# A four-layer graph network: where layer 2's load buffers lie, and what its first two chunks begin with

## The chip, the cores and the metric

The kernel runs on one core of one Trainium2 chip. The metric is the device time of the whole program in microseconds (us), as a median over runs. The kernel before has a median of 1073.51 us over 3 runs (1072.81 to 1073.6).

The engines are named as in the profile: PE (TensorE), DVE (VectorE), ACT (ScalarE), POOL (GpSimd) and SP (SyncE, which here issues most DMAs). Each engine works through its own instructions in order; semaphores tie the engines together.

## The reference

`x` is 2708 x 128 and `adj` is 2708 x 2708, both float32; about 0.6% of `adj` is not zero. Each of the four layers normalises the rows of `x`, applies a ReLU to give `h`, and adds a graph layer to `x`. Layers 0 and 1 are a mean over neighbours and a message network with GELU for each edge. The layers that the change touches are 2 and 3:

```python
# layer 2
agg = adj @ states                       # states is h
msg = relu(agg @ W_msg.T + b_msg)
x = x + gru_cell(msg, states)            # gates r, z and candidate n
# layer 3, for each of two heads
mask = (adj > 0) | eye(n)
h = x_norm @ ff0_w[i].T
e = where(mask, leaky_relu(s_src[:, None] + s_dst[None, :]), NEG)
att = softmax(e, axis=1) @ h + x
```

## The kernel before, in words

The 2708 rows are held as 22 row tiles of 128 rows (`NT = 22`; the last has 20). Columns are taken in chunks of four tiles, 512 columns (`GROUPS`: five of these and one of 148 columns).

**Layer 0** reads `adj` once, lists the non-zero values of each row (`val`, `col`) and writes the transposed matrix to `adjT` in DRAM. **Layer 1** works from the lists: `period(t)` handles row tile t, with gathers by matmul, a GELU, and sums; `updates` (line 697) does the steps that end a group of four tiles, up to `hs`, the normalised rows that layer 2 multiplies. Its memory is held by pools that are open until `lists.close()`: `val`, `col`, `later`, `xb` and others in `keep`, scratch in `fix`, `once` and more. The order of instructions in layer 1 and in layer 2 is that of the code (`manual_schedule`). After layer 1's last update, DVE works out from the lists whether any row had more entries than the lists hold (`lost1`, `over1`, `many`), and puts that into `flag`.

**Layer 2** is `aggregate` and `finish_chunk`. For each chunk of columns, `aggregate` is called for pieces of five row tiles (`PIECE = 5`: four pieces of 1.28 MB, and a last one of the remaining two tiles, 256 KB and 40 KB). It loads the piece from `adjT` on SP's queue (L1082, L1084) into one of three buffers `a2` of pool `l2a`; lets DVE make the mask (`a > 0`, kept for layer 3) of the first four row tiles (L1086) and POOL that of the fifth (L1089); and gives PE one matmul for each row tile into the PSUM sum `p_agg` (L1094). A fourth load can be issued only when both masks and the matmuls of the first piece have been done.

`finish_chunk` is a generator. It copies the sum (`aggc`, L1105), turns `h` (`p_h2`, `hc`), puts the diagonal into the mask (L1112, four DVE operations), and does the GRU: p_m and `msg` (L1115, L1117), p_hn and `half_n` (L1121, L1123), the gates (L1125 to L1130), p_in (L1131), `nn` on DVE and ACT (L1134 to L1138), `y2` on DVE (L1142 to L1144), p_y back to rows (L1150) and into `xs` (L1156), two layer norms (`n3`, whose `h` rows ACT scales at L137, and `n3z`, `z`), p_z (L155, L1171) and p_hv, `hv` (L1179, L1185). Its pool `l2g` has one buffer for each tag, and `aggc` shares tag `t2` with `nn`, `half_n` shares `t1` with `y2`. The sums lie in PSUM tags acc0 and acc1 in turn, the gates in acc2 to acc5.

When a chunk's sum is done, `follow(finish_chunk(...))` hands the generator to a small planner. Each matmul of `aggregate` spends `n / CH` units of a clock (1 for 512 columns); `advance()` lets each generator run on when the units that it yielded have passed. So the finishing of one chunk is laid, at build time, between the matmuls of the next. `late_weights` (L379 to L388, among it p_w on PE and `w_x` on DVE) runs after the first chunk's sum.

**Layer 3** takes `row`, `hv`, `lift` and the mask, weighs on DVE (L923) and multiplies on PE (L955). Its tiles (pool `l3`) are allocated right after `lists.close()`; a first instruction on POOL is the memset of `score` (L887).

Of the kernel before, what the change touches and what calls it, by code (L numbers as in the profile page):

```python
# [20 lines left out]
F32 = mybir.dt.float32  # L21
BF16 = mybir.dt.bfloat16
AF = mybir.ActivationFunctionType
ALU = mybir.AluOpType
AX = mybir.AxisListType
U16 = mybir.dt.uint16
I32 = mybir.dt.int32
U8 = mybir.dt.uint8
PSUM = bass.MemoryType.PSUM

P = 128
N = 2708
D = 128
NT = (N + P - 1) // P
FULL = N // P
TAIL = N - FULL * P
CH = 512
# [7 lines left out]
NB = (N + JB - 1) // JB  # L45
S = 8
E = P
GROUPS = [(t, min(4, NT - t)) for t in range(0, NT, 4)]
# [3 lines left out]
def size(t):  # L52
    return min(P, N - t * P)
# [7 lines left out]
def listed_layers(ctx: ExitStack, tc: tile.TileContext, x, adj, w, out, flag):  # L61
    nc = tc.nc
# [100 lines left out]
    keep = lists.enter_context(tc.tile_pool(name="keep", bufs=1))  # L163
    val = keep.tile([P, NT, NB, S], F32, name="val")
    col = keep.tile([P, NT, NB, S], U16, name="col")
    own = keep.tile([P, NT], F32, name="own")
    total = keep.tile([P, NT], F32, name="total")
    inv = keep.tile([P, NT], F32, name="inv_deg")

    HB = NB // 2  # L170
    HP = 8
    R = 4
    C = 4 * S + R + 1

    count = keep.tile([P, P], F32, name="count")
    nc.gpsimd.iota(count, [[1, P]], base=0, channel_multiplier=0, allow_small_or_imprecise_dtypes=True)
# [9 lines left out]
    rows_n = keep.tile([P, NT, NB], BF16, name="rows_n")  # L186
    ends = keep.tile([P, NT, NB], BF16, name="ends")
    some4 = keep.tile([P, 4, NB, S], BF16, name="some4")
    later = keep.tile([P, NB, E], BF16, name="later")
    nc.gpsimd.memset(later, 0.0)  # L190
    xb = [keep.tile([P, NB, C], BF16, name=f"xb{q}") for q in range(2)]
    for q in range(2):
        nc.gpsimd.tensor_copy(xb[q][:, :, 4 * S : 4 * S + R], part.unsqueeze(1).to_broadcast([P, NB, R]))

# [184 lines left out]
    def late_weights():  # L379
        nc.vector.tensor_tensor(gate_b, b_ih[:, 0:2], b_hh[:, 0:2], ALU.add)  # L380
        nc.vector.tensor_scalar(gate_b, gate_b, 0.5, None, ALU.mult)
        nc.vector.tensor_scalar(half_b, b_hh[:, 2:3], 0.5, None, ALU.mult)
        nc.vector.tensor_copy(w_x[:, 0 : 2 * D], ff0T)
        for k in range(2):
            p = bank("p_w")[:, 0:2]
            nc.tensor.matmul(p, ff0[:, k, :], attn[:, 2 * k : 2 * k + 2], start=True, stop=True)
            nc.vector.tensor_copy(w_x[:, 2 * D + k : 2 * D + k + 1], p[:, 1:2])
            nc.vector.tensor_copy(w_x[:, 2 * D + 2 + k : 2 * D + 3 + k], p[:, 0:1])  # L388
# [6 lines left out]
    with (  # L395
# [56 lines left out]
        def list_late(t):  # L452
            units = state.pop(("late", t), [])
            for n, b, a in units:
                nc.vector.max(val[0 : size(n), n, b, :], a)
            for n, b, a in units:
                nc.vector.max_index(col[0 : size(n), n, b, :], val[0 : size(n), n, b, :], a)
# [251 lines left out]
        def period(t, between=()):  # L709

            now, c, b, a = (0 <= t + q < NT for q in range(4))
            last = 0 <= t - 1 < NT
            if c and not between:
                put_values(t + 1)
            for k in range(GB):
                for step in between[k : k + 1]:
                    step()
                if now:
                    combine(t, k)
                    activate(t, k)  # L720
                if k < 2:
                    if last:
                        gather(t - 1, GB - 2 + k)
                    if k == 0 and c:
                        pass_on(t + 1)
                    if k == 1 and a:
                        rank(t + 3)
                    if k == 1 and last:
                        close_tile(t - 1)
                elif now:  # L730
                    gather(t, k - 2)
                if k in (1, 2) and b:
                    fetch(t + 2, k - 1)
                if k == 1 and a:
                    describe(t + 3)
                if k == 2:
                    if now and t % 2 == 0 and t + 2 < NT:
                        sources(t // 2 + 1)
                    if a:
                        select_rows(t + 3)  # L740
                    if now and t + 4 < NT:
                        count_rows(t + 4)
                    updates(t)
                if k > 0 and c:
                    put_more(t + 1, k)
                if k == 3 and c:
                    columns(t + 1)
                if k == 3 and b:
                    place(t + 2)
                if k == 4 and a:  # L750
                    finish_rows(t + 3)
                if k == 4:
                    load_late(t + 1)
                if k == GB - 1:
                    list_late(t)


        def spread_sums(g):
# [63 lines left out]
        def put_rest(t):  # L822
            for k in range(1, GB):
                put_more(t, k)

        with tc.manual_schedule():
            for step, n in (
                (spread_sums, 0), (spread_sums, 1), (rank, 0), (enter, 0),
                (select_rows, 0), (describe, 0), (enter, 1), (spread_sums, 2), (rows, 0), (turn_rows, 0),
                (rows, 1), (destinations, 0), (turn_rows, 1),  # L830
                (finish_rows, 0), (fetch_both, 0), (rank, 1), (enter, 2), (spread_sums, 3), (select_rows, 1),
                (split_destinations, 0), (destinations, 1), (describe, 1), (rows, 2), (turn_rows, 2),
                (place, 0), (pass_on, 0), (sources, 0), (enter, 3), (spread_sums, 4), (split_destinations, 1),
                (destinations, 2), (rows, 3), (turn_rows, 3), (finish_rows, 1), (fetch_both, 1), (enter, 4),
                (spread_sums, 5), (columns, 0), (place, 1), (split_destinations, 2), (destinations, 3), (rows, 4),
                (turn_rows, 4), (enter, 5), (rank, 2), (select_rows, 2), (rows, 5), (turn_rows, 5), (describe, 2),
                (split_destinations, 3), (put_values, 0), (destinations, 4), (put_rest, 0), (finish_rows, 2),
            ):
                step(n)

            def fourth():
                split_destinations(4)
                destinations(5)

            def fifth():
                split_destinations(5)
                put_values(1)

            period(0, (fourth, fifth))
            for t in range(1, NT + 1):  # L850
                period(t)
            for t in range(NT + 1, NT + 1 + STEPS):
                updates(t)


        lost = fix.tile([P, 3, NT], F32, name="lost1")
        nc.vector.reduce_sum(lost[:, 0, :], rows_n, AX.X)
        nc.vector.tensor_scalar(lost[:, 1, :], own, 0.0, None, ALU.is_gt)
        nc.vector.tensor_scalar(lost[:, 2, :], own, 0.0, None, ALU.is_lt)
        nc.vector.tensor_tensor(lost[:, 0, :], lost[:, 0, :], lost[:, 1, :], ALU.add)  # L860
        nc.vector.tensor_tensor(lost[:, 0, :], lost[:, 0, :], lost[:, 2, :], ALU.subtract)
        nc.vector.tensor_tensor(lost[:, 0, :], lost[:, 0, :], total, ALU.not_equal)
        nc.vector.reduce_sum(flag, lost[:, 0, :], AX.X)
        over = fix.tile([P, 2], F32, name="over1")
        many = once.tile([P, NT, NB], BF16, tag="picked", name="many")
        nc.vector.tensor_tensor(many, ends, rows_n, ALU.add)
        nc.vector.tensor_scalar(many, many, float(E), None, ALU.is_gt)
        nc.vector.reduce_sum(over[:, 0:1], many, AX.XY)
        nc.vector.tensor_scalar(many, val[:, :, :, S - 1], 0.0, None, ALU.is_gt)
        nc.vector.reduce_sum(over[:, 1:2], many, AX.XY)  # L870
        for q in range(2):
            nc.vector.tensor_tensor(flag, flag, over[:, q : q + 1], ALU.add)
    lists.close()


# [1 line left out]

    l3 = ctx.enter_context(tc.tile_pool(name="l3", bufs=1))  # L880
    h3 = l3.tile([P, NT, D], F32, name="h3")
    mask = l3.tile([P, NT, N], U8, name="mask")
    hv = l3.tile([P, NT, 2, D + 1], F32, name="hv")
    lift = l3.tile([P, NT, 2], F32, name="lift")
    row = l3.tile([P, 2, N], F32, name="row")
    score = l3.tile([P, NT, 4], F32, name="score")
    nc.gpsimd.memset(score[:, NT - 1, :], 0.0)  # L887
    ident_8 = l3.tile([P, P], U8, name="ident_8")
    nc.vector.tensor_copy(ident_8, ident)
    PIECE = 5  # L890
    RUNS = ((0, 3), (3, 8), (11, 8), (19, 3))
# [175 lines left out]
            yield apart  # L1067

    with (
        tc.tile_pool(name="l2a", bufs=3) as apool,  # L1070
        tc.tile_pool(name="l2g", bufs=1) as pool,
        tc.tile_pool(name="l2z", bufs=2) as zpool,
        tc.tile_pool(name="l3v", bufs=4) as vpool,
# [26 lines left out]
        def finish_chunk(t0, k0, pa):  # L1100
# [103 lines left out]
            for k in range(2):  # L1204
# [2 lines left out]
                    passed[k * k0 : (k + 1) * k0, :].rearrange("t i -> (t i)")[0:n].partition_broadcast(P),  # L1207
                )

        for g, (t0, k0) in enumerate(GROUPS):  # L1210
            pa = accs.tile([P, CH], F32, tag=f"acc{g % 2}", name="p_agg")
            for j0 in range(0, NT, PIECE):
                aggregate(t0, k0, pa, j0)
            if t0 == 0:
                late_weights()
            follow(finish_chunk(t0, k0, pa))
            advance()
        last = RUNS[0]
# [486 lines left out]
```

## Time and profile before

| | |
|---|---|
| median of 3 runs | 1073.51 us (1072.81 to 1073.6) |
| span of the profiled execution | 1069.6 us |
| median less that span | 3.9 us |
| PE busy in the span | 950.0 us (89%) |
| DVE, ACT, POOL busy | 824.4, 515.4, 398.7 us |
| layer 1's last update matmul (p_u) ends | 614.87 us |
| layer 2's matmuls (p_agg) | 620.98 to 774.0 us |
| mean granted clock of PE | 0.943 |

The profile gives no time of the profiled execution other than its span, from the first to the last instruction; the 3.9 us is the part of the median that lies outside of it, if that execution took as long as the median.

How to read what follows: a line of the waits names the engine and line that waited, what it waited for, the total, how often, and the longest. A line of the timeline begins with start and duration, and ends with the idle time before it and its releaser. A line of the stretches gives length, busy time of PE, PE's weight loads, DVE, ACT and POOL with the number of records, then the granted clock of PE, the share of the DMA engines, and GB/s. A float32 matmul of 512 columns appears as two records.

### The profile page before, as it was taken

Reading aid. Unit: us, or ns where it says so; the run is one execution under the profiler, and the core shown is the slowest. Engines: PE = TensorE matmul, PEld = TensorE weight load, DVE = VectorE, ACT = ScalarE, POOL = GpSimd, SP = SyncE. Lnnn points to the kernel's source line nnn. Section 1 sums busy time; section 2 is a strip of 40 time slices with the busy share of each in tenths; the row PEclk is TensorE's granted clock in tenths of the full one; section 3 lists DMA queues with packets and bytes.
Section 4 is the critical chain, followed back from the end, with each engine's and each line's share of the span. In section 5 each row is a group of like instructions: output and inputs, shape, how many; then the busy total and the mean of one; then the engine's idle time right before and its main releaser. Section 6 shows DMA issues by size and latency. Waiting matters only on the chain. (4 is left out here: it accounts for less than half of the span.)

```text
span 1069.6 us, 21992 instructions
## 1 busy us (share of the span) xinstructions
PE 950.0 (89%) x7950; PEld 754.1 (71%) x7950; DVE 824.4 (77%) x2853; ACT 515.4 (48%) x1428; POOL 398.7 (37%) x476
## 2 busy tenths in 40 slices
PE   5798889934799999999999979999978999999993
PEld 2454445433799999899899934444578999999772
DVE  7999999768577798787878265666578977997673
ACT  7777777634766666666666522433321200320142
POOL 3311112022776656666766163343410300430132
PEclk9999999766799999999999979999989999999996
DMA  9888996221233433322221075566300000000000
GB/s 365 315 303 316 316 342 243 78 65 46 88 109 106 124 95 106 106 91 83 97 96 57 28 256 186 185 225 216 91 22 26 9 1 1 6 15 1 2 15 14
DMA packets 60625, 129.67 MB, mean 121 GB/s; under 512 B 11160, under 2 KB 23828, under 8 KB 57798
## 3 DMA queue, kind: packets, MB, share of 16 engines
q1 hardware_dynamic: 58690, 125.38, 34.2%
q10 hardware_dynamic: 1816, 2.80, 0.8%
q8 instruction: 64, 1.05, 0.4%
q14 instruction: 55, 0.45, 0.1%
HBM read 81.55 MB, written 30.87 MB: 105 GB/s over the span
## 5 line engine op out<-in xcount | busy, mean ns | idle before, releaser
L955 PE MATMUL att<-hv,wt 128*128 128x129 f32 (+2 forms) x1936 | 243.8, 283 | 8.7 <-DVE wt L923 8.7
L955 PEld LDWEIGHTS att<-hv,wt 128*128 128x128 f32 (+2 forms) x1936 | 224.7, 192 | 25.8 <-DVE wt L923 10.1
L923 DVE SCALAR_TENSOR_TENSOR wt<-row,lift,mask 128x1024 f32<-128x1024 f32 (+5 forms) x176 | 160.3, 939 | 34.9 <-PE att L955 34.8
L536 POOL TENSOR_SCALAR put<-mine,value 128x128 f32<-128x128 bf16 x176 | 149.8, 867 | 70.3 <-DVE mine L433 67.9
L612 PE MATMUL p_m<-s,sel 128*128 128x128 bf16 x1452 | 161.6, 220 | 5.4 <-ACT g L624 5.4
L616 PE MATMUL p_m<-d,cols 124*128 124x128 bf16 (+1 forms) x1452 | 161.7, 220 | 1.4 <-DVE cols L566 1.3
L121 POOL TENSOR_TENSOR n_r<-n_r,minus_half 128x4 f32<-128x4 f32 (+1 forms) x31 | 46.1, 1486 | 286.5 <-DVE n_r L120 280.9
L637 PE MATMUL agg<-put,g 128*128 128x128 f32 (+1 forms) x968 | 135.9, 281 | 0.0
L297 PE MATMUL acc<-a,hs 128*128 128x512 f32 (+2 forms) x264 | 124.4, 574 | 10.8 <-ACT hs L137 10.8
L309 PEld LDWEIGHTS p_T<-ident,a 128*128 128x128 f32 x484 | 60.1, 144 | 88.3 <-issue 40.3
L637 PEld LDWEIGHTS agg<-put,g 128*128 128x128 f32 x968 | 118.2, 192 | 0.0
L1094 PE MATMUL p_agg<-a,hs 128*128 128x512 f32 (+2 forms) x264 | 109.3, 556 | 7.3 <-DMA a<-adjT 7.2
L612 PEld LDWEIGHTS <-sel 128*128 128x128 bf16 x1452 | 104.3, 98 | 10.8 <-issue 7.0
L285 DVE FIND_INDEX8 col<-val,a 128x8 uint16<-128x124 f32 (+1 forms) x400 | 108.1, 285 | 0.0
L309 PE MATMUL p_T<-ident,a 128*128 128x128 f32 x484 | 82.3, 289 | 26.2 <-ACT aT L313 19.4
L624 ACT ACTIVATE g<-p_m 128x512 f32<-128x512 f32 x132 | 73.1, 554 | 63.8 <-PE p_m L616 63.8
L616 PEld LDWEIGHTS <-cols 124*128 124x128 bf16 (+1 forms) x1452 | 102.5, 98 | 1.9 <-DVE cols L566 1.9
L544 ACT ACTIVATE put<-mine,value 128x128 f32<-128x128 bf16 x308 | 100.5, 391 | 0.0
L283 DVE MAX8 val<-a 128x8 f32<-128x124 f32 (+1 forms) x400 | 92.8, 276 | 2.5 <-DMA a<-in_adj 2.5
L313 ACT ACTIVATE aT<-p_T 128x512 f32<-128x512 f32 (+2 forms) x132 | 71.1, 541 | 47.9 <-ACT aT L313 32.7
L1094 PEld LDWEIGHTS p_agg<-a,hs 128*128 128x128 f32 (+1 forms) x264 | 47.5, 194 | 55.8 <-issue 54.2
L297 PEld LDWEIGHTS acc<-a,hs 128*128 128x128 f32 (+1 forms) x264 | 44.7, 202 | 25.9 <-issue 14.8
(252 smaller groups left out, 1418.7 us busy)
## 6 DMA issues: line engine op xcount, KB each, us to landing
a<-in_adj SPq DMA_DIRECT2D x21, 1354.0 KB
adjT<-aT SPq DMA_DIRECT2D x105, 256.0 KB
a<-adjT SPq DMA_DIRECT2D x20, 1280.0 KB
spread<-passed SPq DMA_DIRECT2D x22, 704.0 KB
later<-sel SPq DMA_DIRECT2D x22, 616.0 KB
row<-own_d ACTq DMA_DIRECT2D x10, 256.0 KB
later<-sel SPq DMA_DIRECT2D x22, 82.5 KB
adjT<-aT SPq DMA_DIRECT2D x21, 74.0 KB
```

The lines of the kernel that those rows point to most:

```text
L283: nc.vector.max(val[:, n, b, :], block(b))
L285: nc.vector.max_index(col[:, n, b, :], val[:, n, b, :], block(b))
L297: nc.tensor.matmul(accs[ci][:, 0:cw], h[0:m, n, :], sets[n // 4][0:m, n % 4, c : c + cw], start=(n == 0), stop=(n == NT - 1),)
L309: nc.tensor.transpose(p[0:k, q * P : q * P + m], sets[gi][0:m, q, j * P : j * P + k], ident[0:m, 0:m])
L536: nc.gpsimd.tensor_scalar(st["put", 0][:, b, :], st["mine"][:, b, :], st["value"][:, b : b + 1], None, ALU.mult)
L544: nc.scalar.activation(st["put", 1][:, b - HP, :], st["mine"][:, b, :], AF.Identity, scale=st["value"][:, b : b + 1])
L612: nc.tensor.matmul(p[:, b - b0, :], st["sel"][:, b, :], s3[:, q, t % 2, :], start=(q == 0), stop=False)
L616: nc.tensor.matmul(p[:, b - b0, :], st["cols"][0:kb, b, :], d3[0:kb, b, q, :], start=False, stop=(q == 2))
L637: nc.tensor.matmul(agg, g[:, b - 4 * k, :], put, start=(b == 0), stop=False)
L923: nc.vector.scalar_tensor_tensor(wt[0:kj, :], row[0:kj, k, c : c + n], lift[0:kj, j, k : k + 1], mask[0:kj, j, c : c + n], op0=ALU.max, op ...
L955: nc.tensor.matmul(banks[s // 3][0:m, s % 3, :], wt[0:kj, q * P : q * P + m], hv[0:kj, j, k, :], start=(v < 2 and s // 3 not in touched), ...
L1094: nc.tensor.matmul(pa[:, 0:n], h[0:k, j, :], a[0:k, j - j0, 0:n], start=(j == 0), stop=(j == NT - 1))
```

## The change: where the buffers lie, and the order of the pieces

Three parts.

1. Memory. Pool `l2a` gets `reuse_waits="tile"`, so that each buffer waits only for the earlier users of its own bytes, and `l3` gets this too and is allocated from the other end of memory (`side="right"`). In `keep`, `later` and `xb` are placed directly behind `val` and `col`; in `l3`, `mask` goes last. By the built program, the three `a2` buffers then lie over `val`, `col`, `later` and `xb` (bytes 51808 to 82528 of a partition; before, 167712 to 198432), and `mask` at 169760 to 229336.
2. The check of the lists (16 DVE operations) becomes a function, and is called in `period(NT - 3)` where it stood behind layer 1 before.
3. Chunks 0 and 1 both take their four whole pieces (20 row tiles) first; then come `late_weights`, the last piece of chunk 0, `follow(finish_chunk)` for it, the last piece of chunk 1, and its `finish_chunk`. The other chunks are as before.

```diff
+    later = keep.tile([P, NB, E], BF16, name="later")
...
+    xb = [keep.tile([P, NB, C], BF16, name=f"xb{q}") for q in range(2)]
+    own = keep.tile([P, NT], F32, name="own")
...
                 if k == GB - 1:
                     list_late(t)
+                    if t == NT - 3:
+                        check_lists()
...
+        def check_lists():
+            lost = fix.tile([P, 3, NT], F32, name="lost1")
+            nc.vector.reduce_sum(lost[:, 0, :], rows_n, AX.X)
...
+            nc.vector.tensor_scalar(many, val[:, :, :, S - 1], 0.0, None, ALU.is_gt)
+            nc.vector.reduce_sum(over[:, 1:2], many, AX.XY)
+            for q in range(2):
+                nc.vector.tensor_tensor(flag, flag, over[:, q : q + 1], ALU.add)
...
-    l3 = ctx.enter_context(tc.tile_pool(name="l3", bufs=1))
+    l3 = ctx.enter_context(tc.tile_pool(name="l3", bufs=1, side="right", reuse_waits="tile"))
     h3 = l3.tile([P, NT, D], F32, name="h3")
-    mask = l3.tile([P, NT, N], U8, name="mask")
...
+    mask = l3.tile([P, NT, N], U8, name="mask")
...
-        tc.tile_pool(name="l2a", bufs=3) as apool,
+        tc.tile_pool(name="l2a", bufs=3, reuse_waits="tile") as apool,
...
+        def sums_of(g):
+            return accs.tile([P, CH], F32, tag=f"acc{g % 2}", name="p_agg")
+
+        pieces = list(range(0, NT, PIECE))
+        first = [sums_of(g) for g in range(2)]
+        for g in range(2):
+            for j0 in pieces[:-1]:
+                aggregate(*GROUPS[g], first[g], j0)
+        late_weights()
         for g, (t0, k0) in enumerate(GROUPS):
-            pa = accs.tile([P, CH], F32, tag=f"acc{g % 2}", name="p_agg")
-            for j0 in range(0, NT, PIECE):
+            pa = first[g] if g < 2 else sums_of(g)
+            for j0 in pieces[-1:] if g < 2 else pieces:
                 aggregate(t0, k0, pa, j0)
-            if t0 == 0:
-                late_weights()
             follow(finish_chunk(t0, k0, pa))
             advance()
```

More of the change, by code (lines that the diff above doesn't have):

```diff
@@ L165, in listed_layers @@
     col = keep.tile([P, NT, NB, S], U16, name="col")
-    own = keep.tile([P, NT], F32, name="own")
-    total = keep.tile([P, NT], F32, name="total")
-    inv = keep.tile([P, NT], F32, name="inv_deg")
+    later = keep.tile([P, NB, E], BF16, name="later")
     HB = NB // 2
@@ L173, in listed_layers @@
     C = 4 * S + R + 1
+    xb = [keep.tile([P, NB, C], BF16, name=f"xb{q}") for q in range(2)]
+    own = keep.tile([P, NT], F32, name="own")
+    total = keep.tile([P, NT], F32, name="total")
+    inv = keep.tile([P, NT], F32, name="inv_deg")
     count = keep.tile([P, P], F32, name="count")
@@ L188, in listed_layers @@
     some4 = keep.tile([P, 4, NB, S], BF16, name="some4")
-    later = keep.tile([P, NB, E], BF16, name="later")
     nc.gpsimd.memset(later, 0.0)
-    xb = [keep.tile([P, NB, C], BF16, name=f"xb{q}") for q in range(2)]
     for q in range(2):
@@ L824, in put_rest @@
                 put_more(t, k)
+        def check_lists():
+            lost = fix.tile([P, 3, NT], F32, name="lost1")
+            nc.vector.reduce_sum(lost[:, 0, :], rows_n, AX.X)
+            nc.vector.tensor_scalar(lost[:, 1, :], own, 0.0, None, ALU.is_gt)
+            nc.vector.tensor_scalar(lost[:, 2, :], own, 0.0, None, ALU.is_lt)
+            nc.vector.tensor_tensor(lost[:, 0, :], lost[:, 0, :], lost[:, 1, :], ALU.add)
+            nc.vector.tensor_tensor(lost[:, 0, :], lost[:, 0, :], lost[:, 2, :], ALU.subtract)
+            nc.vector.tensor_tensor(lost[:, 0, :], lost[:, 0, :], total, ALU.not_equal)
+            nc.vector.reduce_sum(flag, lost[:, 0, :], AX.X)
+            over = fix.tile([P, 2], F32, name="over1")
+            many = once.tile([P, NT, NB], BF16, tag="picked", name="many")
+            nc.vector.tensor_tensor(many, ends, rows_n, ALU.add)
+            nc.vector.tensor_scalar(many, many, float(E), None, ALU.is_gt)
+            nc.vector.reduce_sum(over[:, 0:1], many, AX.XY)
+            nc.vector.tensor_scalar(many, val[:, :, :, S - 1], 0.0, None, ALU.is_gt)
+            nc.vector.reduce_sum(over[:, 1:2], many, AX.XY)
+            for q in range(2):
+                nc.vector.tensor_tensor(flag, flag, over[:, q : q + 1], ALU.add)
         with tc.manual_schedule():
@@ L853, in listed_layers @@
                 updates(t)
[L856 to L872, printed above, removed]
     lists.close()
-    l3 = ctx.enter_context(tc.tile_pool(name="l3", bufs=1))
+    l3 = ctx.enter_context(tc.tile_pool(name="l3", bufs=1, side="right", reuse_waits="tile"))
     h3 = l3.tile([P, NT, D], F32, name="h3")
-    mask = l3.tile([P, NT, N], U8, name="mask")
     hv = l3.tile([P, NT, 2, D + 1], F32, name="hv")
```

## Prediction, made before the run

> **What bounds the kernel now.** I read the waits of TensorE between 600 and 775 us first, then a table of stretches, then the timeline. The waits (line waited for: us in total, times, longest):
>
> ```profile
> PE p_agg L1094 <- DMA a<-adjT: 7.2, 2, 6.1
> PE p_y L1150 <- DVE hv L1185: 0.5, 2, 0.3
> PE p_hv L1179 <- DVE hv L1185: 0.5, 1, 0.5
> ```
>
> Layer 2 is bound by TensorE: beyond two waits for loads at its start, next to nothing. The stretches (length, PE busy; the last three columns are granted clock, DMA share, GB/s):
>
> ```profile
> 614.87:620.98 6.11, 0.00 (x1) 0.03 (x1) 3.92 (x22) 2.37 (x6) 1.84 (x2) 0.50 0.81 283
> 620.98:636.75 15.77, 15.77 (x30) 6.58 (x30) 10.34 (x30) 2.52 (x6) 12.19 (x11) 0.83 0.61 218
> 636.75:637.86 1.11, 0.00 (x1) 0.03 (x1) 0.47 (x3) 0.00 (x0) 0.59 (x2) 1.00 0.92 343
> 644.30:774.00 129.70, 128.47 (x385) 63.42 (x385) 79.92 (x220) 45.73 (x127) 50.43 (x32) 1.00 0.56 185
> ```
>
> TensorE idles 6.11 us for the first load, runs 15 matmuls (30 records) partly at half clock, idles 1.11 for the fourth load, and from 644.3 works 128.5 of 129.7 us. A microsecond gained or lost before 774 therefore reaches the end. Why the loads come when they do, from the waits of SP's queue and the timeline (start, duration):
>
> ```profile
> SPq L1082 <- PE p_u L672: 21.1, 1, 21.1
> ```
>
> ```profile
> 628.08 0.72 POOL L692 TENSOR_TENSOR u<-u,ln_b 128x256 f32<-128x256 f32 x1
> 628.83 0.43 DVE L694 TENSOR_TENSOR xs<-xs,u 128x256 f32<-128x256 f32 x1 [0.82 <-POOL u L692]
> ...
> 629.37 0.10 POOL L887 MEMSET score<- 128x4 f32 x1 [0.57 <-DVE xs L694]
> 629.45 7.15 POOL L1089 TENSOR_SCALAR mask<-a 128x512 uint8<-128x512 f32 x3
> ...
> 630.33 1.20 DVE L1086 TENSOR_SCALAR mask<-a 128x2048 uint8<-128x2048 f32 x1
> ```
>
> SP waited 21.1 us for layer 1's last matmul. The fourth load needs a buffer back, so it waits for both masks of piece 1; these stand in their queues behind layer 1's last steps (L692 to 628.80, L694 to 629.26).
>
> **What the Trainium skill says.** "TensorE: Matmul & The Clock Gate", Part 1, "What's actually happening": half clock after an idle window of about 3.4 us, full again after about as long busy. The trace agrees roughly: after 6.11 idle the clock is 0.50 up to about 626.3, 5.3 us of work; a gap of 2.74 at 775.4 halved it too, one of 1.11 didn't. Same page, "Architectural detail": ACT and DVE are strict FIFO. The trace shows it: masks behind L694. "SBUF — State Buffer", "Who interferes with whom": GpSimd and some DVE operations lock each other out. L1089 takes 1.48 to 3.18 us, which fits. [...] the trace has 5.8 from issue (632.02) to use (637.80), which I take.
>
> **The change part by part.**
>
> *Early loads.* Their memory is free after the check of the lists and the last use of `xb`, so the three loads follow the last `spread` at about 589.5 and have landed by about 603. They could delay that `spread` (issued 589.11, wanted 592.80) and so the columns made from it; but it is ahead of them in SP's queue, and columns (592.80 to 593.75) are needed only at 596.6. Zero; at worst 1 without that cover. SP itself then waits before load 4, with only further layer 2 loads behind it.
>
> *The moved check.* 16 DVE operations, 3.9 us, move one period or so ahead. In the built order they lie where DVE sat 6.77 us before 592.80: zero. Without that cover at most 3.9, and only if PE waited. The memset of `score` waits for p_u alone, so POOL's first mask starts about 0.5 earlier, 628.9. `late_weights` (0.6 of PE) only changes place.
>
> *Start of p_agg.* DVE reads p_u until 616.77, so PE starts at 616.85, 4.1 earlier than 620.98. Its 15.77 of work ends at 632.6. But load 4 still waits for DVE's first mask, 630.33 to 631.53: issue 631.6, use 631.6+5.8=637.4, against 637.86 before. PE waits about 5 us there. So the 4.1 moves from one gap into another; **gain 0.45**. And now the gap that falls here is long enough for half clock: before, the cold 5.3 us ended at 626.3, all hidden under load 4. Now another 5.3 us run at half, at most +2.65, none if the clock stays; I take **+2.2**. Pieces 4 to 8 then take 25 matmuls of 0.86 = 21.5 and PE is the bound (a load takes 3.4 of transfer, both masks below 3.2, a piece 4.3).
>
> *The two finishing chains side by side.* Before, `finish_chunk(0)` ran beside the 25 matmuls of chunk 1, and so on. Now chunk 1 has only its tail left (2 matmuls) when chunk 0 begins to finish; both chains run at once, in program order on each queue, on pool l2g's single buffers. I walked the built order through by hand from T0, the end of the 40 matmuls. Durations from chunk 0 before: ACT L1105 0.57, half_n and gates 0.69, tanh 0.72; each DVE operation of `nn` and `y` 0.69; mask 1.22; the four diagonal masks 0.89.
>
> PE's order from T0, with 0.86 for a 512-column matmul (two records) and 0.5 for four transposes: p_w to 0.6, chunk 0's tail (2 matmuls) to 2.25, p_h(0) to 2.75, half of chunk 1's tail to 3.6, then the six matmuls p_m(0) to p_in(0), the first waiting for aggc(0) and hc(0), the later ones for msg (0.69), to 9.6; the other half of the tail to 10.45, p_h(1) to 10.95, one matmul of chunk 2 to 11.8.
>
> (A) p_m(1), next, wants aggc(1), which shares tag t2 with nn(0). That is free after y(0): nn add to 10.3, DVE's diagonals and mask to 12.4, three y operations to 14.6, ACT's copy and handovers to 15.65. **Stall 3.85** (bounds 2.0 without the diagonals and mask between, 4.5). Before, p_y(0) stood behind 6 matmuls (5.31), and nothing of the next chunk's chain wanted its buffers for 29 us. Half clock afterwards: 0 to 2.65, taken **+1.7**.
>
> (B) half_n(1) shares t1 with y(0), free after p_y(0) at 23.0. Then half_n 0.7, gates 1.4, nn 1.4 and tanh 0.7, with xs(0) and its BN (2.6) ahead on DVE, y(1) 2.1: p_y(1) at 31.0. PE's queue ahead of it, 4 matmuls, ends at 26.45. **Stall 4.55** (2.9 to 5.5).
>
> (C) 11 matmuls to 40.95, then p_z(0), whose z(0) stands on ACT behind h(0) and h(1). Chain on DVE, POOL and ACT: xs(1), BN 1.9, factors 1.3 and POOL 1.9, twice over with masks between, h 1.65 each, z 1.65: 44.55. With hand-over times uncertain, **+3.1** (0 to 5). Cold clock after B lies within it.
>
> (D) p_z(1), hv of chunk 1 and a table load (1.28) in turn: **+1.8** (0 to 2.5). (E) p_h(2) behind it: **+0.6** (0 to 0.8). The waits in the table above for hv, about **0.5**, go.
>
> Later chunks run as before and PE has no slack to win it back; layer 3's order is unchanged.
>
> **Sum:** -0.45+2.2+3.85+1.7+4.55+3.1+1.8+0.6-0.5 = 16.85. The profiled execution spans 1069.6; the median of 1073.51 (1072.81 to 1073.6) holds 3.9 outside the span, which stays. 1073.51+16.85 = 1090.4; I say **1090**. All lower ends give +4.0 (1077.5), all upper ends +23.2 (1096.7); together they aren't likely, so this case holds 1079 to 1096.
>
> **The rivals.**
> - *The finishing chains are hidden.* PE's other matmuls cover A to D as they did one chain before. For: 44 matmuls of chunks 2 and 3 are at hand, and ACT is busy only 46 of 129.7 us. Against: shared tags and in-order queues, and `finish_chunk` has matmuls that nothing may overtake. What stays: -0.45+2.2+0.6 = +2.3, **1075.9**.
> - *Faster.* The start's 4.1 is kept: this needs load 4 issued before about 626.5 (landing by 632.3), or its wait short, and chains hidden. For: 6.11 is by far the largest wait, and early loads remove it. Against: piece 1's masks stand behind L692 and L694, at 628.8. It decides from the moment that those masks finish 5 us sooner. -4.1: **1069.4**.
> - *The waits hold.* If the loads still wait for p_u (a byte of layer 1 under them), the start is as before and the chains hidden: **1073.5**.
>
> **How the numbers follow.** Stalls 0.75, hidden chains 0.10, faster 0.09, waits hold 0.06. About 0.2%, 2.1 us, is what a measurement can tell from no change. Hidden chains fall to 0.04 same and 0.06 slower; so faster 0.09, same 0.10, slower 0.81. The range needs the hidden case too: 1075 to 1097 holds about 0.72+0.09.
>
> **What would show it.** Start: three loads issued at about 589.5; the 6.11 gap about 2.0; p_agg's second gap, at piece 4, about 5 instead of 1.11, with clock 0.50 behind it. Chains: waits of p_m for aggc, of p_y for y and of p_z for z of 3 to 5 us each between 665 and 710. From chunk 3 on, 29 us a chunk as before. Wrong if load 4 is issued before 628, or if PE is over 98% busy between 660 and 710; then a rival has it. Wrong in size if DVE's mask doesn't stand between nn(0) and y(0): A falls to 2.0.

## The result, and the profile after

| | before | after |
|---|---|---|
| median | 1073.16 us (4 runs, 1071.84 to 1073.6) | 1090.11 us (4 runs, 1086.13 to 1092.54) |
| ratio | | 1.0153, 95% interval 1.0126 to 1.0179 |
| span of the profiled execution | 1069.6 us | 1084.3 us (its time: 1086.13 us) |
| DVE's last read of p_u to layer 3's first `att` | 616.77 to 778.10: 161.33 us | 618.48 to 796.69: 178.21 us |

Slower by 17 us. Single runs of one kernel differ by several us (before, over 33 runs in a later comparison: 1066.19 to 1076.04), and so do layers 1 and 3 of the profiles. Layer 1 ends 1.7 us later in the profile after. But over the eleven profiles of this document it ends between 615.05 and 618.48 us, and the two with the old layer 1 have 616.77 and 615.05: neither the moved check nor the early loads show there. Layer 3 takes 3.9 us less in the profile after (from the first `att` on 287.6 us, against 291.5), while the other profiles with the same memory have 289 to 292. So I compare layer 2 by itself, from DVE's last read of p_u to the first `att`: +16.88 us. The four lines, two of before and two of after:

```profile
616.50 0.27 DVE L678 TENSOR_TENSOR u<-p_u,upd_b 20x128 f32<-20x128 f32 x1
778.10 2.92 PE L955 MATMUL att<-hv,wt 128*128 128x129 f32 x12 [2.74 <-DVE wt L923]
...
618.21 0.27 DVE L677 TENSOR_TENSOR u<-p_u,upd_b 20x128 f32<-20x128 f32 x1
796.69 2.90 PE L956 MATMUL att<-hv,wt 128*128 128x129 f32 x12 [2.67 <-DVE wt L924]
```

The waits of TensorE between 600 and 800 us, after. Lines of the new code are one or two numbers off those of before (p_agg is L1095, p_y L1151):

```profile
PE p_agg L1095 <- DMA a<-adjT: 6.0, 1, 6.0
PE p_y L1151 <- DVE y L1145: 4.0, 1, 4.0
PE p_z L155 <- DVE hv L1186: 3.7, 1, 3.7
PE p_m L1116 <- ACT aggc L1106: 3.0, 1, 3.0
PE p_agg L1095 <- issue: 2.7, 1, 2.7
```

Where layer 2 had two waits, for loads, it now has five. The gap at the start is 2.7 us ("issue": it ends 0.1 us after DVE's read of p_u); the second gap for a load is 6.0 where it was 1.1; and three waits of 3 to 4 us are new. The timeline of SP and of the two masks of piece 1:

```profile
591.11 0.35 SPq L557 DMA_DIRECT2D spread<-passed  x1
591.50 54.88 SPq L1083 DMA_DIRECT2D a<-adjT  x7
...
630.53 6.78 POOL L1090 TENSOR_SCALAR mask<-a 128x512 uint8<-128x512 f32 x3
632.06 1.64 DVE L1087 TENSOR_SCALAR mask<-a 128x2048 uint8<-128x2048 f32 x1
633.84 12.54 SPq L1083 DMA_DIRECT2D a<-adjT  x4
```

The first loads follow right behind the last `spread`, 23 us earlier than before. (The x7 joins all issues up to 646.38; the fourth is the first of the x4 in the last line.) It is issued at 633.84, when DVE's first mask ends (633.70), as before. The stretches of layer 2, cut at each gap (length, PE busy, PE's loads, DVE, ACT, POOL, then granted clock):

```profile
618.57:633.73 15.16, 15.16 (x30) 6.38 (x30) 9.81 (x39) 4.59 (x11) 9.40 (x10) 0.86 0.00 1
633.73:639.69 5.96, 0.01 (x2) 0.03 (x1) 4.04 (x10) 0.67 (x2) 4.34 (x4) 0.72 0.81 280
639.69:662.96 23.27, 23.27 (x51) 10.22 (x52) 6.92 (x9) 0.21 (x1) 15.19 (x7) 0.92 0.70 237
...
675.43:678.40 2.97, 0.00 (x1) 0.00 (x0) 2.16 (x4) 0.63 (x2) 0.00 (x0) 1.00 0.97 340
678.40:689.41 11.01, 11.01 (x28) 4.87 (x28) 1.98 (x3) 3.49 (x6) 0.00 (x0) 1.00 0.06 24
689.41:693.42 4.01, 0.00 (x1) 0.00 (x0) 3.75 (x13) 0.21 (x1) 2.01 (x2) 1.00 0.94 308
693.42:709.84 16.42, 16.30 (x40) 7.37 (x40) 13.37 (x51) 5.96 (x14) 10.14 (x7) 0.90 0.32 103
709.84:713.53 3.69, 0.00 (x1) 0.03 (x1) 0.75 (x3) 3.07 (x11) 2.53 (x2) 1.00 0.81 249
713.53:719.94 6.41, 6.41 (x14) 2.84 (x14) 1.82 (x7) 1.36 (x7) 1.49 (x1) 0.60 0.30 80
```

Behind three of these four gaps the clock of the next row is below 1: 0.92, 0.90 and 0.60; behind the gap of 2.97 it is 1.00. In the 23.27 us of the third row 25 matmuls ran, which take 21.5 at full clock (0.86 each).

### The profile page after: what moved, and what is told of

Read it like the earlier page. It is cut to its first block, busy times and chain, and to the rows that moved or that the text cites. A ratio compares the mean times of both kernels' runs of the same rounds, so it can differ in the third digit from the quotient of the medians.

```text
span 1084.3 us, 21990 instructions
## 1 busy us (share of the span) xinstructions
PE 952.4 (88%) x7950; PEld 751.5 (69%) x7950; DVE 823.5 (76%) x2853; ACT 515.3 (48%) x1428; POOL 396.5 (37%) x476
## 5 line engine op out<-in xcount | busy, mean ns | idle before, releaser
L956 PE MATMUL att<-hv,wt 128*128 128x129 f32 (+2 forms) x1936 | 239.3, 280 | 8.7 <-DVE wt L924 8.7
L956 PEld LDWEIGHTS att<-hv,wt 128*128 128x128 f32 (+2 forms) x1936 | 220.7, 189 | 25.0 <-DVE wt L924 12.8
L1095 PE MATMUL p_agg<-a,hs 128*128 128x512 f32 (+2 forms) x264 | 113.2, 573 | 8.7 <-DMA a<-adjT 6.0
L284 DVE FIND_INDEX8 col<-val,a 128x8 uint16<-128x124 f32 (+1 forms) x400 | 110.8, 298 | 0.0
L282 DVE MAX8 val<-a 128x8 f32<-128x124 f32 (+1 forms) x400 | 96.0, 291 | 2.0 <-DMA a<-in_adj 2.0
L1095 PEld LDWEIGHTS p_agg<-a,hs 128*128 128x128 f32 (+1 forms) x264 | 48.9, 200 | 58.5 <-issue 50.9
```

Source lines behind the costliest of these rows:

```text
L282: nc.vector.max(val[:, n, b, :], block(b))
L284: nc.vector.max_index(col[:, n, b, :], val[:, n, b, :], block(b))
L956: nc.tensor.matmul(banks[s // 3][0:m, s % 3, :], wt[0:kj, q * P : q * P + m], hv[0:kj, j, k, :], start=(v < 2 and s // 3 not in touched), ...
L1095: nc.tensor.matmul(pa[:, 0:n], h[0:k, j, :], a[0:k, j - j0, 0:n], start=(j == 0), stop=(j == NT - 1))
```

## The experiments

Theory 1: the loss is that of two finishing chains at once (single buffers, queues in order, PSUM banks), about 14.5 us, and of the gap at the start, which only moved, about 2. Theory 2: the memory, the waits on its bytes and the moved check cost; the order is harmless. Theory 3, on the stalls alone: the in-order queues of DVE and ACT make them, whatever the buffers are. Ratios below are to the kernel before, with 95% intervals.

**The old order of the chunks, on the new memory.**

```diff
         for g, (t0, k0) in enumerate(GROUPS):
-            pa = first[g] if g < 2 else sums_of(g)
-            for j0 in pieces[-1:] if g < 2 else pieces:
+            pa = accs.tile([P, CH], F32, tag=f"acc{g % 2}", name="p_agg")
+            for j0 in range(0, NT, PIECE):
                 aggregate(t0, k0, pa, j0)
+            if t0 == 0:
+                late_weights()
```

> Memory and the moved check as changed, chunk order as before. Theory 1 (the two finishing chains side by side cost some 14.5 us, the moved gap at the start some 2): the waits of p_m for aggc, p_y for y and p_z for hv go; the gap before piece 4 stays about 6 with half clock behind it, +1.8. About 1075, between 1073 and 1077. Theory 2 (it is the memory and the waits on its bytes that cost): about 1088, with the loss still there.

1073.76 us, 1.0018 (1.0001 to 1.0035). Its stretches at the start:

```profile
615.56:630.76 15.20, 15.19 (x30) 6.37 (x30) 9.88 (x39) 4.59 (x11) 9.44 (x10) 0.86 0.00 1
630.76:636.52 5.76, 0.00 (x1) 0.03 (x1) 4.00 (x10) 0.51 (x2) 4.29 (x4) 0.73 0.81 282
636.52:645.30 8.78, 8.78 (x18) 3.70 (x18) 2.73 (x8) 0.83 (x2) 5.44 (x3) 0.79 0.54 180
645.30:778.70 133.40, 128.70 (x385) 63.51 (x384) 84.08 (x236) 46.05 (x130) 50.59 (x33) 1.00 0.54 179
```

The gap of 5.76 and the low clock behind it are there, the three stalls of the chains are gone. (The trace's waits put this gap down to ACT's late rows of h; but DVE and POOL begin the masks of the same piece at 636.40 and 636.46, as its load lands, and the spare loads below pass without a gap.) Layer 2 by the measure above takes 163.24, 1.9 more than before. Theory 2 falls. And the early loads gain nothing by themselves: the stretch is 1.9 us longer, and the medians 0.2%, with an interval that begins just above 1.

**The new order alone, on the old memory.** The kernel before, with the loops that end the diff.

> The kernel before, with the chunk order of the change alone. Theory 1: first gap 6.1, second about 1.1 and no half clock behind it; then the stalls 3.0 + 4.0 + 3.7 and two stretches of half clock of about 1.9 and 2.7: about 1073.2 + 14.5 = 1087.7. Theory 2: about 1073.

1086.64 us, 1.0130 (1.0100 to 1.0159); the waits:

```profile
PE p_agg L1094 <- DMA a<-adjT: 8.1, 2, 6.2
PE p_y L1150 <- DVE y L1144: 4.0, 1, 4.0
PE p_z L155 <- DVE hv L1185: 3.7, 1, 3.7
PE p_m L1115 <- ACT aggc L1105: 3.0, 1, 3.0
```

The three stalls come with the order, to a tenth of a microsecond. Memory and check alone cost 0.18%, the order alone 1.30%: together nearly the 1.53% of the change. One detail was expected wrongly: the second gap here is 1.98, not 1.1, and the clock halves behind it (636.15 to 659.54 takes 23.39 at a mean clock of 0.93). This profile, of the slowest of the four runs, has 181.54 us in layer 2, 3.3 more than that of the change.

**Own memory for each step of the chain.**

```diff
-            nn = pool.tile([D, CH], F32, tag="t2", name="nn")
+            nn = half_n
-            y = pool.tile([D, CH], F32, tag="t1", name="y2")
+            y = hc
```

> As changed, but nn is written over half_n and y over hc (which has two buffers), so that aggc and half_n of the next chunk share memory with neither. Theory 1 (shared single buffers make the stalls): p_m's wait for aggc falls from 3.0 to about 0.6; p_y's wait for y from 4.0 to about 1.7, with no half clock behind it; p_z's 3.7 with its half clock stays. About 1090 - 6.5 = 1083.5. Theory 3 (the in-order queues of DVE and ACT make them, whatever the buffers): stalls move but keep their sum, about 1089.

1081.48 us, 1.0078 (1.0053 to 1.0103), where the change has 1.0153; the waits that belong to the chains:

```profile
PE p_z L155 <- DVE hv L1186: 3.7, 1, 3.7
...
PE p_z L155 <- ACT z L137: 1.4, 1, 1.4
PE p_y L1151 <- DVE hc L1145: 1.3, 1, 1.3
```

The wait for aggc is gone, that for y has fallen from 4.0 to 1.3, and a wait for chunk 0's z of 1.4, which the delay had hidden, appears. Sum 6.4, of 10.7: theory 1 for two of the stalls. The 1.3 + 1.4 that are left may be the queues' (theory 3); this isn't shown. By the ratios this run is 8 us faster than the change, where 6.5 were expected; layer 2 of its profile takes 174.46, which is 3.8 less.

**Two loads into memory that nobody uses yet.**

```diff
+        spare = {
+            (0, 3 * PIECE): part_of(hv.rearrange("p t k d -> p (t k d)")),
+            (GROUPS[1][0], 0): part_of(h3.rearrange("p t d -> p (t d)")),
+        }
...
-            a = apool.tile([P, PIECE, CH], F32, name="a2")
+            a = spare.get((t0, j0))
+            if a is None:
+                a = apool.tile([P, PIECE, CH], F32, name="a2")
```

> As changed, but piece 4 of chunk 0 and piece 1 of chunk 1 are loaded into memory of hv and h3, which nobody uses until later, so that these loads wait for no mask: issued at about 612. Theory 1: no gap before piece 4 (6.0) and no half clock behind it (1.8); the 40 matmuls end about 7.7 earlier, 1082.4. If what holds PE there is the masks or late rows of h instead, a gap stays and it gives less than 3.

1081.78 us, 1.0078 (1.0057 to 1.0098). Both loads are issued at 610.4 and 610.8, and PE goes through:

```profile
616.91:632.37 15.46, 15.46 (x31) 6.88 (x32) 10.13 (x39) 4.59 (x11) 9.69 (x10) 0.85 0.13 47
632.37:655.00 22.63, 22.63 (x57) 9.98 (x55) 12.65 (x24) 0.88 (x2) 18.36 (x10) 1.00 0.58 201
```

From the first p_agg to p_w (the end of the 40 matmuls) 36.76 us pass (616.91 to 653.67), against 44.39 after the change (618.57 to 662.96): 7.6 less, 7.7 expected. The masks are late, but only the buffers tie them to PE. Layer 2 as a whole takes 174.00 in this profile, only 4.2 less: half clock took back 1.7 us behind p_m's stall (12.70 against 11.01) and 1.3 behind p_z's (705.94 to 716.35, 10.41 us; 713.53 to 722.68, 9.15 us, after the change).

**The second chain later.**

```diff
                 aggregate(t0, k0, pa, j0)
+                if g == 2 and j0 == pieces[2]:
+                    follow(finish_chunk(*GROUPS[1], first[1]))
+                    advance()
-            follow(finish_chunk(t0, k0, pa))
-            advance()
+            if g != 1:
+                follow(finish_chunk(t0, k0, pa))
+                advance()
```

> As changed, but finish_chunk of chunk 1 begins only after 15 matmuls of chunk 2 (7 before the next chunk's chain). Theory 1 (two chains at once, on single buffers and in-order queues, make the stalls): p_m's wait for aggc and p_y's wait for y go, p_z's falls or goes; the gap at the start stays: 1090 less about 12, near 1078. If simply the place of chunk 1's sums costs: no change, 1090.

1075.62 us, 1.0054 (1.0032 to 1.0076). The gap of 6.0 stays, the waits for aggc and y are not on the list, p_z waits 0.7, and the longest new ones are 2.0 (p_row) and 1.0 (p_h). With the same sums in the same order, distance between the chains is enough to remove the stalls of 3 to 4 us. Layer 2 still takes 168.30, 7.0 more than before: the gap at the start and the smaller waits stay.

**Matmuls in the gap.**

```diff
+                if (g, j0) == (0, pieces[3]):
+                    warm = bank("p_warm")
+                    for q in range(6):
+                        nc.tensor.matmul(warm, h[:, q, :], h[:, 0:4, :].rearrange("p t d -> p (t d)"), start=(q == 0), stop=(q == 5))
                 aggregate(*GROUPS[g], first[g], j0)
```

> As changed, with six more matmuls of 512 columns on hs, whose result is not used, ahead of piece 4 of chunk 0: 5.2 us of work inside the gap of 6.0. If the half clock behind that gap costs 1.8: the 25 matmuls of pieces 4 to 8 take 21.5 instead of 23.3, and the end comes 1.8 earlier (too little for the medians, readable in the trace). If they cost for another reason (masks, loads), 23.3 stays.

1085.21 us, 1.0113 (1.0091 to 1.0135). The timeline of PE:

```profile
632.21 5.31 PE L1221 MATMUL p_warm<-hs 128*128 128x512 f32 x12
638.36 21.70 PE L1095 MATMUL p_agg<-a,hs 128*128 128x512 f32 x50 [0.84 <-DMA a<-adjT]
```

The 25 matmuls from piece 4 on end in p_w at 659.89, after 21.53 us instead of 23.27. The half clock behind the gap costs 1.74 us: with the gap filled, the 25 matmuls take what they take at full clock. (By the ratios the run is 4 us faster than the change; the intervals overlap and don't settle how much of that is chance.)

**PSUM for p_hv.** Which thing made p_z of chunk 1 wait 3.7?

```diff
-                p = bank("p_hv")
+                p = accs.tile([P, CH], F32, tag=f"acc{4 + q % 2}", name="p_hv")
```

> As changed, but p_hv has PSUM tags acc4 and acc5 and not the two banks that p_z, p_y and p_h share. If p_z's wait of 3.7 is for those banks, held by p_hv until ACT's exponentials behind z and the table load have been done: p_z(1) then waits for z alone, about 1.3, and part of the rest comes back at the third p_hv: 1 to 2.4 us less. If it is ACT's order alone (z behind h, table load, exponentials), the sum of the waits there stays 3.7.

1084.25 us, 1.0104 (1.0075 to 1.0134). In the waits:

```profile
PE p_hv L1180 <- DVE hv L1186: 1.1, 1, 1.1
PE p_hv L1180 <- DVE nn L1138: 0.5, 1, 0.5
...
PE p_z L155 <- ACT z L137: 0.2, 1, 0.2
```

3.7 has become 0.2, with 1.1 and 0.5 back at p_hv, and p_z itself takes 1.48 instead of 0.63, as its transposes follow z piece by piece. It was the two PSUM banks: p_z no longer waits for hv. Chunk 0's p_hv held both until ACT's exponentials, which stand behind z(1) and the table load, and DVE's products were done. What it is worth in time stays open: the profile of this run shows no gain in layer 2 (179.3 us by the measure above), with half clock after p_m's stall, where the change's profile had none.

**Both repairs.** Spare loads, and only piece 1 of chunk 1 ahead of chunk 0's last piece, so that 17 matmuls stand between the chains:

```diff
-        for g in range(2):
-            for j0 in pieces[:-1]:
-                aggregate(*GROUPS[g], first[g], j0)
+        for j0 in pieces[:-1]:
+            aggregate(*GROUPS[0], first[0], j0)
+        aggregate(*GROUPS[1], first[1], 0)
         late_weights()
...
-            for j0 in pieces[-1:] if g < 2 else pieces:
+            for j0 in pieces[-1:] if g == 0 else pieces[1:] if g == 1 else pieces:
```

> As changed, with the two loads into memory of hv and h3 of the run before, and only piece 1 of chunk 1 ahead of chunk 0's last piece, so that 17 matmuls stand between the two finishing chains and not 2. Theory 1: no gap before piece 4, and the waits for aggc, y and hv of 3 to 4 us are gone; PE does 5 matmuls of chunk 1 (4.3 us) ahead of chunk 0's sum. Against the kernel before: start 3.4 earlier after layer 1's last matmul, the 1.1 gap gone, a half-clock stretch of equal length: about -5, 0.995 of before. If the stalls come from the chunk order as such, waits of 3 us or more stay and it is slower than before.

1064.09 us, 0.9916 (0.9899 to 0.9933): faster than both kernels. Its waits in layer 2:

```profile
PE p_agg L1105 <- issue: 2.1, 1, 2.1
PE p_rz L1140 <- ACT msg L1128: 0.8, 1, 0.8
```

Layer 2 takes 154.24 by the measure above (617.86 to 772.10), 7.1 less than before; 5 were expected. p_w, behind piece 1 of chunk 1, comes 25.3 us after p_u, where p_w of the kernel before came after 29.4 without that piece.

Then the 2.1 at the start, which had no cause in the data: PSUM pool `l23p` as a whole waited for p_u.

```diff
-    accs = ctx.enter_context(tc.tile_pool(name="l23p", bufs=1, space=PSUM))
+    accs = ctx.enter_context(tc.tile_pool(name="l23p", bufs=1, space=PSUM, reuse_waits="tile"))
```

> The staggered version with two spare loads, and the PSUM pool of the sums given waits on its own bytes too (reuse_waits tile on l23p), so that p_agg need not wait for DVE's last read of p_u: the 2.1 us between p_u and p_agg go. Late rows of h (tiles 20, 21) are ready about 24 us after p_u and then stand close to the last piece of chunk 0, so some of it may come back: 1 to 2 us less than the staggered version, about 0.990 of before. If rows of h hold it: the same as the staggered version.

1061.92 us, 0.9907 (0.9881 to 0.9934), not told apart from the run before. p_agg now starts with p_u's end, but 1.9 come back as waits for late rows of h and 0.8 at p_h:

```profile
PE p_agg L1105 <- ACT hs L137: 1.9, 2, 1.3
PE p_h L155 <- DVE w_x L387: 0.8, 1, 0.8
```

From p_u's end to `att` it is 155.7 us against 156.3 for the run with both repairs: 0.6 of the 2.1, below the 1 to 2 expected.

## Why the prediction was right, and where its terms were off

The direction, the cause and the total were right: 16.85 forecast, 16.88 measured in layer 2 and 16.95 in the medians. That the total is so close is partly luck: the interval of the ratio spans 13.5 to 19.2 us, and the terms were less good than their sum:

| term | predicted | measured | from |
|---|---|---|---|
| start to piece 4 | -0.45 | +0.1 | 639.69-618.48 against 637.86-616.77 |
| half clock, pieces 4 to 8 | +2.2 | +1.8 | 23.27-21.5; the run with matmuls in the gap |
| A, p_m for aggc | +3.85 | +2.97 | waits |
| half clock behind A | +1.7 | 0 | clock 1.00 after |
| B, p_y for y | +4.55 | +4.01 | waits |
| C, p_z of chunk 0 | +3.1 | +0.7 within p_z; +1.7 half clock behind B | p_z waits for z piece by piece, 1.17 to the next matmul (705.06 to 706.23), 0.44 before (672.46 to 672.90); p_y and 11 matmuls take 11.8 after, 10.1 at full clock in the run with own memory |
| D, p_z of chunk 1 | +1.8 | +3.69, and +3.1 half clock | 713.53 to 722.68 less a wait of 0.25: 8.9; the same work at full clock in the run with matmuls in the gap, 712.17 to 718.66 less 0.68: 5.8 |
| E, small waits | +0.6 | +0.7 | waits: 0.3, 0.2, 0.2 |
| waits of before that go | -0.5 | -1.5 | waits of before: 0.5, 0.5, 0.3, 0.2 |
| sum | 16.85 | 17.3 | 16.88 by the stretch; the 0.4 between stays open |

- **Start.** Right. Load 4 came with DVE's first mask, and from its issue to its use 5.85 us passed (633.84 to 639.69), where 5.8 were taken. The 0.5 expected didn't come: DVE's mask began as long after layer 1 as before (632.06-618.48 = 13.6 against 630.33-616.77 = 13.6), and took 1.64 instead of 1.20. The spare loads showed the reason: without the tie to the masks, 7.6 us come back.
- **Early loads beside the last spread, and the moved check.** Costed at zero, with worst cases of 1 and 3.9: the time from the spread's issue to `cols` grew from 3.69 to 4.50 us (591.11 to 595.61; 4.03 with the old memory in the run of the order alone). The p_m wait for cols is 1.2, as before (1.3), so it was covered. DVE did the check from 584.56 to 589.39, and still sat idle for 5.19 us ahead of `cols`.
- **A and B.** The shared tags were the cause, as forecast; both were over-sized, by 0.9 and 0.5. Counted from p_w's start (662.96), PE came to A at 12.5 and not at 11.8, and went on at 15.4, not at 15.65. It came to B at 26.45 as forecast, but y(1) was ready 0.5 earlier, at 30.46 and not at 31.0. (The walk says six matmuls from p_m(0) to p_in(0); there are seven, and its 6.0 us are those of seven.)
- **C and D.** The step that failed. I had let chunk 0's z be late by 3.1 and given chunk 1's p_z only 1.8. The half clock behind B let PE arrive late enough for most of z(0), and the long wait was chunk 1's p_z, not for z but for a PSUM bank. The forecast had listed hv and the table load there, and had not seen that p_hv and p_z share two banks. Size and place were off; the sum C+D was 4.9 against 9.2 with both half-clock stretches.
- **Half clock.** Taken behind A, where it didn't come in this run; put within C's 3.1 behind B, where it came; and left out behind D, where it came too. In the runs of the order alone, of the spare loads, of the matmuls in the gap and of the PSUM for p_hv it did come behind A (12.65, 12.70, 12.70 and 13.92 us for the same work as 11.01), so this term varies from run to run by up to 2.9 us.
- **The 3.9 us outside the span.** In every run of which both are known, the time is 1.7 to 2.0 us longer than the span, so the profiled execution of before was some 2 us faster than the median. The forecast, a difference added to the median, isn't touched.
- **The rivals.** That the chains are hidden is refuted by the three waits; that the start's 4.1 is kept, by the gap of 6.0. It needed load 4 before 626.5: with it the gap is gone, and with the chains apart as well the whole is 0.9916.

## What to carry to other kernels

A load that arrives early is worth only as much as the next one behind it: look at what the first buffer's return waits for before moving the first load. Work of the next stage that is drawn ahead of a chain of latency also draws the next chain up to it; keep the distance between two chains as long as their shared buffers and PSUM banks are held, or give them their own. And when a gap on TensorE moves, count the half clock behind it as part of its price.

## What the runs showed of the hardware that was not expected

The gap after which TensorE's clock halves has no fixed length here. The first `att` of layer 3, 12 records after a gap of 2.65 us, in the run with the old order and then in the one with both repairs:

```profile
778.70 1.61 PE L956 MATMUL att<-hv,wt 128*128 128x129 f32 x12 [2.65 <-DVE wt L924]
```

```profile
772.10 2.95 PE L956 MATMUL att<-hv,wt 128*128 128x129 f32 x12 [2.65 <-DVE wt L924]
```

The same work behind the same gap takes 1.61 or 2.95 us. Chunk 1's p_z shows it too, after the change and then in the run with matmuls in the gap:

```profile
713.53 0.63 PE L155 MATMUL p_z<-ident,z 128*128 128x128 f32 x4 [3.69 <-DVE hv L1186]
...
717.84 2.10 PE L1180 MATMUL p_hv<-w_x,z3T 128*128 128x260 f32 x4
```

```profile
712.17 0.63 PE L155 MATMUL p_z<-ident,z 128*128 128x128 f32 x4 [3.70 <-DVE hv L1186]
...
715.08 1.14 PE L1180 MATMUL p_hv<-w_x,z3T 128*128 128x260 f32 x4
```

Two p_hv take 2.10 us, or 1.14 at full clock, and it is the longer gap that has full clock behind it. A gap of 1.98 had half clock behind it in the run of the order alone, and none in that of the later second chain (p_row; clock 1.00 in the next 6.49 us). One of 2.97 or 2.98 had it in four runs and not in the profile of the change; gaps of 1.11 and 1.32 had none. This fits a window that runs on by itself, as the Trainium skill ("TensorE: Matmul & The Clock Gate", Part 1, "What's actually happening") describes it; but its idle time of about 3.4 us is more than the gaps of 1.98 to 2.98 that were enough here. That it also moves whole runs is not shown: the same layer 3 takes 291.5 and 287.6 us in the profiles of before and after, with mean clocks of 0.93 and 0.97 in its first 62 us.
